# An f32 mixture-of-experts layer: products 4 and 5 of the first layer in seven blocks each, the second layer's first sum in its accumulator, and another order for the rotation

## The chip, the cores and the metric

One core of a Trainium2 chip. The time is device microseconds of one execution; below, one is a profiled execution, and three are plain runs. Engines are named as in the profile: PE is TensorE (PEld its weight loads), DVE is VectorE, ACT is ScalarE, POOL is GpSimd, SP is SyncE, which here only issues DMAs.

## The reference

4096 tokens of 512 features, f32. Each token is rotated by quaternions (a fixed 4x4 mixing M of its four groups of 128 features, with per-channel weights), sent to two of eight experts with at most 1024 slots each, passed through a two-layer network there, weighted, and added to the input.

```python
rot = cond(x)                              # quaternion rotation of the features
scores = softmax(rot @ gate_w.T)           # top 2 of 8, gates normalised
de = dispatch(rot)                         # (8 experts, 1024 slots, 512)
h  = relu(einsum('ecd,ehd->ech', de, fc1_w) + fc1_b)    # hidden size 2048
eo = einsum('ech,ehd->ecd', h, fc2_w) + fc2_b
out = x + sum_k gate_k * eo[slot of (token, k)]
```

## The kernel before

The first 80 us route the tokens. After that there are 32 stages k = (expert e, group g of 512 hidden units, g = 0 to 3). Of a stage both layers are block products of a 2x2 split, done with seven block products (numbered 0 to 6) in place of eight: the left factors are sums of weight blocks (`left1`, POOL), the right ones sums of blocks of the rotated tokens (`Slots.factors`, POOL, once an expert) or of second-layer weights (`right2`, POOL), and the products are added into the four result blocks by DVE and ACT.

**First layer** (`layer1`, L846). A product is 256x256 by 256x512. Products 0, 5 and 4 are done whole (`half`, L858): four f32 matmuls of 512 columns, each two records in the trace. Products 1 and 6, and then 3 and 2, are split once more into seven half blocks each, and done in pairs (`pair`, L878, with matmuls of 256 columns at L837 in `within`). The sums that these need come from `left_sub` (L146; four POOL operations of 128x128, L155 to L158) and `right_sub` (L162; four DVE operations of 128x256 on tile `xsub`, L170 to L173, once an expert). In the list of seven factors that each returns, entries 0, 1 and 3 on the left are raw blocks, 2, 4, 5 and 6 are sums; on the right 0, 1 and 2 are raw. The results collect in SBUF, in `beside` (h11, h21, r12) and h22: PSUM banks are added on by DVE (L892 for both halves of a bank, L905 for a bank added twice, L911, L929, L921), ACT writes the first ones with the bias and does the relus. `chain` (L811) then makes the second layer's remaining left factors s1, s2, r12 and, by `last`, s4, in DVE operations of 128x1024 (L823, L824, L825, L820).

**Second layer** (`second_layers`, L1124). For each pair of slot tiles (st0 = 0 and 2) seven products of eight matmuls of 256 columns (`product2`, L796, L800). `start` does product 0 of the next pair ahead, and adds it to the old accumulator into a tile v1 of its own. The accumulators `acc0` and `acc2` have one buffer; at an expert's first stage a new one is taken, ahead of o11, the first write.

**Order.** Nothing is scheduled automatically: every engine does its instructions in the order in which the program emits them. Two generators alternate (L1251 on): one unit of `layer1` of stage k, then one unit of the second layer of stage k - 1. I call such a pair a turn; 14 make a stage, turn i having unit i. The second layer's units for st0 = 0 lie in turns 3 to 9, those for st0 = 2 in turns 10 to 13 and, of the next stage, 0 to 2: `start` is in turns 7 and 0. After each unit `turn(n)` takes n operations from `background` (the chain, at its front; the rotation of the next expert's tokens, `Slots.steps`; weights and `Rows.store` of finished rows) and one from `fetches` (DMAs). How many is in PACE, by stage and turn. A store is an ACT scaling (L671), a POOL add onto the row (L673) and a POOL scatter (L657). POOL also gathers rows (L601, `gather_rows`, eight from turn 3 of g = 0 on), choices (L633, in g = 3), and the next expert's tokens (L694, `gather_ahead`), which SP then exchanges between partitions (`exchange`, 16 small DMAs for each part).

`first_layers` (L982) says when the sums are emitted: `TURN_OF_SUM` gives the turn of each of the four sums of the next stage's left factors (the order 2, 0, 1, 3 in turns 8, 9, 10, 13); they overwrite the sums of this stage, so each waits for PE's last use. Before, the sums for products 6 and 1 of stage k + 1 are emitted in turns 9 to 13 of stage k and those for 2 and 3 in turns 2 to 5 of their own stage; the xq gathers of an expert begin in turn 12 of g = 0 and turn 8 of g = 1, its rotation in turn 11 of g = 1 and turn 9 of g = 2.

Of the kernel before, what the change touches and what calls it, by code (L numbers as in the profile page):

```python
# [39 lines left out]
P = 128  # L40
# [26 lines left out]
def kernel(  # L67
# [78 lines left out]
    def left_sub(k, n, block):  # L146

        G = nc.gpsimd
        t = wsum.tile([P, 4, P], F32, tag=f"sub{n}", name=f"sub{n}_{k}")

        def b(m, c):
            return block[:, c, m * P : (m + 1) * P]

        steps = [
            lambda: G.tensor_tensor(t[:, 0], b(1, 0), b(1, 1), ALU.add),  # L155
            lambda: G.tensor_tensor(t[:, 1], t[:, 0], b(0, 0), ALU.subtract),
            lambda: G.tensor_tensor(t[:, 2], b(0, 0), b(1, 0), ALU.subtract),
            lambda: G.tensor_tensor(t[:, 3], b(0, 1), t[:, 1], ALU.subtract),  # L158
        ]
        return [b(0, 0), b(0, 1), t[:, 3], b(1, 1), t[:, 0], t[:, 1], t[:, 2]], steps  # L160
# [417 lines left out]
    vp = ctx.enter_context(tc.tile_pool(name="vp", bufs=1))  # L578
# [35 lines left out]
    beside = [hp.tile([P, 3, 2, HALF], F32, name=f"beside{i}") for i in range(2)]  # L614
    unused = [hp.tile([P, 2, HALF], F32, name=f"hidden{i}") for i in range(5)]
# [60 lines left out]
    class Slots:  # L676
# [37 lines left out]
        def arrivals(self, half):  # L714

            n = PER if half == 0 else 2
            t = self.a if half == 0 else self.b
            for at in range(0, PER, n):
                for st in range(n):
                    yield lambda st=st, at=at: self.gather_ahead(t[:, st], half, at + st)  # L720
                yield from [lambda: None] * 2
                for b in range(QT):
                    yield lambda b=b, at=at: self.exchange(t, half, at, b)
                yield from [lambda: None] * 2
# [71 lines left out]
    def product2(out, st0, factors, n, first, tiles=range(2)):  # L796
# [11 lines left out]
        if st0 + 2 == PER and 1 in tiles and n in (2, 3, 4, 5):  # L808
            unused.append(factors[0][n])

    def chain(k, h22):  # L811


        h11, h21, r12 = (beside[k % 2][:, i] for i in range(3))
# [3 lines left out]
        def last():  # L818
# [7 lines left out]
            *[lambda: None] * (2 if k == NK - 1 else 0),  # L826
            last,
        ]

# [16 lines left out]
    def layer1(k, factors, subs):  # L846
# [5 lines left out]
        h11, h21, r12 = (h[:, i] for i in range(3))  # L852
# [14 lines left out]
        for m in range(2):  # L867
            half(a[m], m, 0, True)
            nc.scalar.activation(h11[:, m], a[m], AF.Identity, bias=lo[:, m : m + 1])
            yield  # L870
        for m in range(2):
            half(a[m], m, 5, False)
            nc.scalar.activation(r12[:, m], a[m], AF.Identity, bias=lo[:, m : m + 1])
            if m == 1:
                nc.scalar.activation(h21[:, m], a[m], AF.Identity, bias=hi[:, m : m + 1])
            yield

        def pair(n, o, at, base, base_read):  # L878

            two = h[:, at : at + 2]
            t, u = bank1(f"t{n}_{k}"), bank1(f"u{n}_{k}")
            halves = t.rearrange("p (n s) -> p n s", n=2)

            def both(bank, i, first=False):
                within(bank[:, A], subs, n, i, first)
                within(bank[:, B], subs, o, i)

            def add(m, half):  # L890
                to = two[:, :, m, half]
                V.tensor_tensor(to, halves, to, ALU.add)  # L892

            within(base[:, A], subs, o, 1)
            within(base[:, B], subs, o, 2)
            base_read()
            both(t, 0, True)
            add(0, A)
            yield
            both(t, 5)  # L900
            add(0, B)
            both(u, 4, True)
            to = two[:, :, :, B]
            term = u.rearrange("p (n s) -> p n s", n=2).unsqueeze(2).to_broadcast([P, 2, 2, HS])
            V.tensor_tensor(to, term, to, ALU.add)  # L905
            yield
            both(t, 6)
            add(1, B)
            within(u[:, A], subs, n, 1, True)
            within(u[:, B], subs, n, 2)  # L910
            V.tensor_tensor(two[:, 0, 0], u, two[:, 0, 0], ALU.add)  # L911
            yield
            both(t, 3)
            add(1, A)
            relu(two[:, 0])

        def from5(m):
            nc.scalar.activation(h21[:, m], a[m], AF.Identity, bias=hi[:, m : m + 1])

        def from4(m):  # L920
            V.tensor_tensor(r12[:, m], b[m], r12[:, m], ALU.add)  # L921

        yield from pair(1, 6, 0, a[0], lambda: from5(0))
        yield
        h22 = unused.pop(0)
        b = [bank1(f"b{m}_{k}") for m in range(2)]
        for m in range(2):
            half(b[m], m, 4, True)
            V.tensor_tensor(h22[:, m], b[m], h21[:, m], ALU.add)  # L929
            if m == 1:  # L930
                from4(1)
                relu(h22)
            yield
        yield from pair(3, 2, 1, b[0], lambda: from4(0))
        chain(k, h22)
# [4 lines left out]
    def layer1_plain(k, w, x):  # L940
# [4 lines left out]
        h11, h21, r12 = (beside[k % 2][:, i] for i in range(3))  # L945
        h22 = unused.pop(0)
        for half in range(2):
# [6 lines left out]
            for at, i in ((at, i) for at in parts for i in range(NJ)):  # L954
# [22 lines left out]
                if half == 1 and done:  # L977
                    chain(k, h22)
# [3 lines left out]
    def first_layers():  # L982
# [43 lines left out]
        TURN_OF_SUM = {8: 2, 9: 0, 10: 1, 13: 3}  # L1026
        nxt = None
        for k in range(NK):
# [27 lines left out]
            if k:  # L1056
                for n, block, turns in (
                    (2, left_f[2], (2, 2, 3, 3)),
                    (3, w1_of[k][:, 1, 1], (4, 4, 5, 5)),
# [3 lines left out]
                if k == 1 or g == 0:  # L1063
                    for n, turns in ((6, (1, 2, 2, 3)), (2, (4, 4, 5, 5)), (3, (6, 7, 8, 9))):
# [5 lines left out]
                units = layer1(k, (left_f, xf), (dict(lefts), right_subs))  # L1070
            else:
                units = layer1_plain(k, w1_next, xs)
            for i, _ in enumerate(units):
# [3 lines left out]
                if k:  # L1077

                    if i == 8 and k + 1 < NK:
                        lefts[6], more = left_sub(k + 1, 6, left_n[6])  # L1080
                        later(more, (9, 10, 11, 12))
                        lefts[1], more = left_sub(k + 1, 1, w1_of[k + 1][:, 0, 1])
                        later(more, (10, 11, 12, 13))
                        if g == NG - 1:
                            right_subs[1], more = right_sub(xtp, e + 1, 1, xf_n[1])
                            later(more, (8, 9, 9, 12))
# [10 lines left out]
                if e + 1 < E:  # L1097

                    if (g, i) in ((0, 12 if e else 5), (1, 8)):
                        fetches.extend(nxt.arrivals(g))  # L1100
                    if (g, i) in ((1, 11), (2, 9)):
# [22 lines left out]
    def second_layers():  # L1124
# [18 lines left out]
        def start(k, st0):  # L1143
            e, g = divmod(k, NG)
            before = biases[e] if g == 0 else accs[st0]
            a = banks(f"a2_{k}_{st0}", (k, st0) == units[-1])
            v1 = vp.tile([P, 2, DB], F32, tag="v", name=f"v1_{k}_{st0}")
# [7 lines left out]
        for n, (k, st0) in enumerate(units):  # L1155
            e, g = divmod(k, NG)
            if g == 0:
                before = biases[e]
                acc = accs[st0] = ap.tile([P, 4, D], F32, tag=f"acc{st0}", name=f"acc{st0}_{e}")
            else:  # L1160
                before = acc = accs[st0]
# [83 lines left out]
        [(1, 1)] * 2 + [(0, 1)] * 4 + [(0, 0)] + [(0, 1)] * 5 + [(1, 1), (0, 0)],  # L1245
        [(1, 1)] * 4 + [(1, 1), (0, 2), (0, 0), (0, 1), (1, 1)] + [(0, 1)] * 3 + [(1, 1), (0, 0)],
        [(1, 1)] * 2 + [(2, 1)] * 2 + [(1, 2), (0, 2), (0, 0), (0, 1), (1, 1)]
        + [(0, 1)] * 3 + [(1, 1), (0, 0)],
# [63 lines left out]
```

## Time and profile before

| | us |
|---|---|
| three runs, median (lowest, highest) | 1566.23 (1565.29, 1566.28) |
| the profiled execution | 1567.49 |
| its span | 1565.7 |
| a stage from k = 2 on | 46.56 (47.12 in g = 2) |
| DVE busy in g = 0, 1, 2, 3 | 35.6, 26.9, 39.7, 39.7 |
| POOL busy in g = 0, 1, 2, 3 | 37.1, 37.7, 21.9, 35.8 |

The profile comes from the profiled execution. Busy is the time in which an engine works on an instruction; POOL's pauses ahead of a DMA that it issues (about 0.3 us) are not in it. A row of instructions gives start, duration, engine, line, operation, output<-inputs, shape; brackets hold the idle time before it and what ended it.

### The profile page before, as it was taken

What the parts mean: (1) busy time and instruction counts of PE and PEld (TensorE: products, weight loads), DVE (VectorE), ACT (ScalarE), POOL (GpSimd) and SP (SyncE); (2) the same over time, 40 slices, a digit from 0 to 9 for tenths busy, and PEclk for the clock granted to TensorE, in tenths of its full rate; (3) what the DMA queues carried; (4) which work ended last, traced back from release to release, by engine and by line L of the source; (5) the groups of instructions that cost most, each with busy time, mean ns of one, the idle gap of its engine ahead of it and who ended that gap; (6) DMA issues with size and microseconds to landing.
All of it is one profiled execution on the core that took longest, in us unless ns stands there. A gap on an engine that the chain in (4) does not pass through costs nothing.

```text
span 1565.7 us, 17505 instructions
## 1 busy us (share of the span) xinstructions
PE 1531.0 (98%) x6399; PEld 1186.9 (76%) x6399; DVE 1152.8 (74%) x1608; ACT 316.6 (20%) x446; POOL 1045.9 (67%) x1129
## 2 busy tenths in 40 slices
PE   5899999999999999999999999999999999999997
PEld 2677777877877777877877777887777877777776
DVE  6667887588866888578885888758886688866656
ACT  3222211211131211221122221221212211121110
POOL 1763687755977478865779567785687747886453
PEclk7899999999999999999999999999999999999999
DMA  8463113421335203441135311442123511321021
GB/s 325 150 215 101 55 61 122 121 81 55 96 106 144 65 28 114 124 118 55 54 95 166 96 55 32 137 130 86 55 79 115 145 41 55 114 94 67 0 82 53
DMA packets 79374, 152.18 MB, mean 97 GB/s; under 512 B 12022, under 2 KB 40950, under 8 KB 74168
## 3 DMA queue, kind: packets, MB, share of 16 engines
q1 hardware_dynamic: 56848, 90.24, 18.6%
q0 software_dynamic: 18048, 52.31, 10.8%
q10 hardware_dynamic: 4392, 8.52, 1.4%
q8 instruction: 50, 0.82, 0.2%
q14 instruction: 36, 0.29, 0.1%
HBM read 119.77 MB, written 25.23 MB: 93 GB/s over the span
## 4 chain that ended last, share of the span: by engine, by line
PE 87%; DVE 6%; DMA 2%; issue 2%; POOL 1%; another core or an unknown queue 1%; SPq 1%; POOLq 0%; DVEq 0%
PE a L800 26%; PE b L800 19%; PE t L837 13%; PE a L858 11%; PE u L837 7%; PE b L858 7%; PE b L837 2%; PE a L837 1%; DMA xb<-in_xt_dram 1%; DVE hidden L824 1%; DVE xa L771 1%; PE p L959 1%; DVE hidden L820 1%; SPq L707 1%
## 5 line engine op out<-in xcount | busy, mean ns | idle before, releaser
L800 PE MATMUL a<-t,hidden 128*128 128x256 f32 x1024 | 242.0, 379 | 0.1
L892 DVE TENSOR_TENSOR beside<-t,beside 128x512 f32<-128x512 f32 x248 | 170.3, 687 | 92.3 <-PE t L837 88.1
L800 PEld LDWEIGHTS a<-t,hidden 128*128 128x128 f32 x1024 | 194.5, 190 | 53.0 <-issue 27.5
L833 ACT ACTIVATE beside<-beside 128x1024 f32<-128x1024 f32 x62 | 65.5, 1057 | 556.8 <-DVE beside L892 535.1
L837 PE MATMUL t<-xsub,sub 128*128 128x256 f32 x496 | 128.1, 381 | 0.9 <-DVE beside L892 0.2
L800 PEld LDWEIGHTS b<-w,hidden 128*128 128x128 f32 x504 | 95.8, 190 | 39.0 <-issue 29.2
L800 PE MATMUL b<-w,beside 128*128 128x256 f32 x512 | 121.0, 379 | 0.6 <-DVE acc L1224 0.6
L800 PE MATMUL a<-t,beside 128*128 128x256 f32 x512 | 120.9, 379 | 0.0
L800 PE MATMUL a<-w,beside 128*128 128x256 f32 x512 | 120.9, 379 | 0.0
L800 PE MATMUL b<-t,hidden 128*128 128x256 f32 x504 | 119.1, 379 | 0.0
L800 PE MATMUL b<-w,hidden 128*128 128x256 f32 x504 | 119.1, 379 | 0.0
L800 PEld LDWEIGHTS b<-w,beside 128*128 128x128 f32 x512 | 97.2, 190 | 27.3 <-issue 15.8
L800 PEld LDWEIGHTS a<-w,beside 128*128 128x128 f32 x512 | 97.3, 190 | 26.4 <-issue 14.8
L858 PE MATMUL b<-x,s 128*128 128x512 f32 x248 | 116.5, 592 | 0.0
L858 PE MATMUL a<-x,s 128*128 128x512 f32 x248 | 116.5, 592 | 0.0
L858 PE MATMUL a<-xa,w 128*128 128x512 f32 x248 | 116.4, 592 | 0.0
L137 POOL TENSOR_TENSOR s<-w 128x512 f32<-128x512 f32 x31 | 39.5, 1274 | 112.5 <-PE b L858 112.5
L139 POOL TENSOR_TENSOR s<-w 128x512 f32<-128x512 f32 x31 | 39.7, 1282 | 109.7 <-PE t L837 109.6
L140 POOL TENSOR_TENSOR s<-w,s 128x512 f32<-128x512 f32 x31 | 39.4, 1272 | 107.5 <-PE t L837 96.7
L800 PEld LDWEIGHTS a<-t,beside 128*128 128x128 f32 x512 | 97.3, 190 | 13.2
L837 PEld LDWEIGHTS t<-xsub,sub 128*128 128x128 f32 x496 | 93.6, 190 | 16.3 <-DVE beside L892 3.4
L800 PEld LDWEIGHTS b<-t,hidden 128*128 128x128 f32 x504 | 95.8, 190 | 13.0
(228 smaller groups left out, 3084.9 us busy)
## 6 DMA issues: line engine op xcount, KB each, us to landing
w<-in_w_dram SPq DMA_DIRECT2D x64, 1024.0 KB
xb<-in_xt_dram SPq DMA_DIRECT2D x8, 1024.0 KB
out_dram<-in_x_dram ACTq DMA_DIRECT2D x1, 8192.0 KB
rows<-xa SPq DMA_DIRECT2D x112, 64.0 KB
rows<-xb SPq DMA_DIRECT2D x224, 32.0 KB
b<-in_b_dram POOLq DMA_DIRECT2D x8, 256.0 KB
c<-choice,slot_cho POOLq DMA_INDIRECT x64
rows<-out_dram,slot_tok POOLq DMA_INDIRECT x64
```

Of the source, the lines that this page charges most:

```text
L137: lambda: G.tensor_tensor(s[0], w[:, 1, 0], w[:, 1, 1], ALU.add),
L139: lambda: G.tensor_tensor(s[2], w[:, 0, 0], w[:, 1, 0], ALU.subtract),
L140: lambda: G.tensor_tensor(s[3], w[:, 0, 1], s[1], ALU.subtract),
L707: nc.sync.dma_start(slots_of[half][q * CW : (q + 1) * CW, at : at + t.shape[1], b * P : (b + 1) * P], t[b * CW : (b + 1) * CW, :, q * P : ...
L771: V.scalar_tensor_tensor(to, t, M[:, i, j : j + 1], to, ALU.mult, ALU.add)
L800: nc.tensor.matmul(out[m] if isinstance(out, list) else out[:, m], lhsT=factors[0][n][:, c, (st0 + m) * P : (st0 + m + 1) * P], rhs=factor ...
L820: V.tensor_tensor(s4, h21, s2, ALU.subtract)
L824: lambda: V.tensor_tensor(s2, s1, h11, ALU.subtract),
L833: nc.scalar.activation(h, h, AF.Relu)
L837: nc.tensor.matmul(out, lhsT=subs[0][n][i], rhs=subs[1][n][i], start=first, stop=True, skip_group_check=True,)
L858: nc.tensor.matmul(out, lhsT=factors[0][n][:, c, m * P : (m + 1) * P], rhs=factors[1][n][:, c, :], start=first and c == 0, stop=c == 1, sk ...
L892: V.tensor_tensor(to, halves, to, ALU.add)
```

## The change

Products 5 and 4 are done by seven blocks as well, one at a time, each with a bank of its own (t5, t4) whose two halves hold two running sums; product 0 alone stays whole. Each half sum is added by one DVE operation to both result columns that it belongs to. h22 moves into `beside`, with a copy of a half of h21 by ACT as its start, and two buffers of `unused` go. The sums for 5 are emitted in turns 0 and 1 and those for 4 in turns 6 and 7 of the stage that uses them; both share a tile. The right sums of 5 and 4 are made with the others in g = 0. v1 goes into the accumulator, which is taken in `start`. `last` is put into the background only when `product2` frees its buffer, in turn 2. The arrivals, the rotation and PACE have new places. The diff, cut:

```diff
-    beside = [hp.tile([P, 3, 2, HALF], F32, name=f"beside{i}") for i in range(2)]
-    unused = [hp.tile([P, 2, HALF], F32, name=f"hidden{i}") for i in range(5)]
+    beside = [hp.tile([P, 4, 2, HALF], F32, name=f"beside{i}") for i in range(2)]
+    unused = [hp.tile([P, 2, HALF], F32, name=f"hidden{i}") for i in range(3)]
...
-        if st0 + 2 == PER and 1 in tiles and n in (2, 3, 4, 5):
+        if st0 + 2 == PER and 1 in tiles and n in (2, 4, 5):
             unused.append(factors[0][n])
+            if n == 2 and waiting:
+                background.insert(0, waiting.pop())
...
+        def add_to_both(two, m, half, term):
+            to = two[:, :, m, half]
+            V.tensor_tensor(to, term.unsqueeze(1).to_broadcast([P, 2, HS]), to, ALU.add)
...
+        two, three = h[:, 0:3:2], h[:, 2:4]
+        t5 = bank1(f"t5_{k}")
+        singles(a[0], 5)
+        nc.scalar.activation(r12[:, 0], a[0], AF.Identity, bias=lo[:, 0:1])
+        within(t5[:, A], subs, 5, 0, True)
         yield
+        singles(a[0], 6)
+        nc.scalar.activation(h21[:, 0], a[0], AF.Identity, bias=hi[:, 0:1])
+        within(t5[:, B], subs, 5, 4)
+        add_to_both(three, 0, A, t5[:, A])
+        yield
+        t, u = bank1(f"t1_{k}"), bank1(f"u1_{k}")
+        within(t5[:, A], subs, 5, 5)
+        add_to_both(three, 0, B, t5[:, A])
+        add_twice_to_both(three, t5[:, B])
+        both(t, 1, 6, 0, True)
+        add(two, 0, A, t)
+        yield
+        within(t5[:, A], subs, 5, 6)
+        add_to_both(three, 1, B, t5[:, A])
+        both(t, 1, 6, 5)
+        add(two, 0, B, t)
+        both(u, 1, 6, 4, True)
+        add_twice(two, u)
+        yield
...
+        nc.scalar.activation(h22[:, 1], h21[:, 1], AF.Copy)
+        singles(b, 4, True)
+        V.tensor_tensor(h22[:, 0], b, h21[:, 0], ALU.add)
...
-        TURN_OF_SUM = {8: 2, 9: 0, 10: 1, 13: 3}
+        TURN_OF_SUM = {8: 2, 11: 0, 12: 1, 13: 3}
+        ARRIVE = (
...
+            {
+                (0, 3): [(0, 0)],
+                (0, 6): [(1, 0)],
+                (0, 13): [(0, 1)],
+                (1, 6): [(1, 1)],
+                (1, 10): [(1, 2)],
+                (1, 13): [(1, 3)],
+            },
...
+                lefts[5], more = left_sub(k, 5, left_f[5], 4)
+                later(more, (0, 0, 1, 1))
-                    (2, left_f[2], (2, 2, 3, 3)),
-                    (3, w1_of[k][:, 1, 1], (4, 4, 5, 5)),
+                    (2, left_f[2], (2, 3, 4, 4)),
+                    (3, w1_of[k][:, 1, 1], (4, 5, 5, 6)),
...
-                    for n, turns in ((6, (1, 2, 2, 3)), (2, (4, 4, 5, 5)), (3, (6, 7, 8, 9))):
+                    for n, turns in (
+                        (5, (0, 1, 2, 3)),
+                        (6, (2, 3, 5, 5)),
+                        (4, (5, 7, 7, 8)),
+                        (2, (8, 10, 10, 11)),
+                        (3, (7, 10, 11, 12)),
+                    ):
...
+                    if i == 6:
+                        its[4], more = left_sub(k, 4, left_f[4])
+                        later(more, (6, 6, 7, 7))
...
-                    if (g, i) in ((1, 11), (2, 9)):
+                    if (g, i) in (((1, 5), (2, 2)) if e else ((1, 11), (2, 2))):
                         background.extend(nxt.steps(g - 1))
...
-            v1 = vp.tile([P, 2, DB], F32, tag="v", name=f"v1_{k}_{st0}")
+            v1 = accs[st0][:, :2, :DB]
...
     PACE = (
-        [(1, 1)] * 2 + [(0, 1)] * 4 + [(0, 0)] + [(0, 1)] * 5 + [(1, 1), (0, 0)],
-        [(1, 1)] * 4 + [(1, 1), (0, 2), (0, 0), (0, 1), (1, 1)] + [(0, 1)] * 3 + [(1, 1), (0, 0)],
-        [(1, 1)] * 2 + [(2, 1)] * 2 + [(1, 2), (0, 2), (0, 0), (0, 1), (1, 1)]
-        + [(0, 1)] * 3 + [(1, 1), (0, 0)],
+        [(1, 1)] * 2 + [(1, 1)] * 4 + [(0, 0)] + [(0, 1)] * 5 + [(1, 1), (0, 0)],
+        [(1, 1)] * 4 + [(0, 0), (1, 1)] + [(0, 1)] * 3 + [(0, 0), (0, 1), (1, 1), (2, 1), (0, 1)],
+        [(1, 1)] * 3 + [(1, 2), (0, 0), (1, 1), (0, 0), (0, 1), (0, 1), (0, 1), (0, 1), (1, 1), (2, 1), (0, 1)],
+        [(1, 1)] * 6 + [(0, 0)] + [(0, 1)] * 4 + [(1, 2)] * 3,
     )
```

`singles(bank, n)` does blocks 1 and 2 of product n into the bank's two halves, `both(bank, n, o, i)` block i of products n and o. Unit 6 does t5's block 3, unit 7 ends the pair 1 and 6; units 8 to 11 do product 4 as 2 to 6 do product 5, beside the pair 3 and 2, which ends in unit 13. The first unit shown in the diff (`singles(a[0], 5)`) is unit 2, and each `yield` ends one. In ARRIVE, of which the table for experts after the first is shown, a key is (g, turn) and an entry (half, part): even parts are gathers, odd ones exchanges.

## The prediction

> **What bounds the kernel now.** I read the page's busy shares first, then its chain, then the stages one by one, then GpSimd's (POOL's) order of work in the stage that is fullest. The page:
>
> ```profile
> PE 1531.0 (98%) x6399; PEld 1186.9 (76%) x6399; DVE 1152.8 (74%) x1608; ACT 316.6 (20%) x446; POOL 1045.9 (67%) x1129
> ...
> PE 87%; DVE 6%; DMA 2%; issue 2%; POOL 1%; another core or an unknown queue 1%; SPq 1%; POOLq 0%; DVEq 0%
> ```
>
> TensorE is the bound. Next, the busy times of four successive stages (a stage is one pass k): g = 3 of expert 4, then g = 0, 1, 2 of expert 5. Columns: the stretch and its length; PE, PEld, DVE, ACT, POOL, each with its number of instructions; clock, DMA share, GB/s:
>
> ```profile
> 919.19:965.75 46.56, 46.56 (x193) 36.42 (x192) 39.73 (x52) 7.19 (x10) 35.81 (x36) 1.00 0.14 46
> 965.75:1012.31 46.56, 46.56 (x193) 36.48 (x192) 35.57 (x49) 9.74 (x14) 37.09 (x38) 1.00 0.35 107
> 1012.31:1058.87 46.56, 46.56 (x193) 36.48 (x192) 26.89 (x35) 12.16 (x18) 37.74 (x43) 1.00 0.49 142
> 1058.87:1105.98 47.11, 46.99 (x193) 36.31 (x192) 39.71 (x51) 9.61 (x14) 21.92 (x27) 1.00 0.25 73
> ```
>
> A stage is 46.56 us of matmuls without a gap; only g = 2 loses 0.56, where the chain of waits passes through VectorE's (DVE's) L824 and L771. So every microsecond taken from TensorE counts, as long as DVE and POOL keep up. POOL has 37 of 46.6 us in g = 0 and 1, not counting the 0.3 us ahead of each DMA it issues. POOL's instructions in time order, at the start of g = 0 and of g = 1:
>
> ```profile
> 965.50 2.36 POOL L128 TENSOR_TENSOR x<-xa,x 128x1024 f32<-128x1024 f32 x1
> 967.82 2.24 POOL L125 TENSOR_TENSOR t<-w 128x512 f32<-128x512 f32 x1
> 970.14 2.20 POOL L126 TENSOR_TENSOR t<-w,t 128x512 f32<-128x512 f32 x1
> ...
> 979.23 0.96 POOL L601 DMA_INDIRECT rows<-out_dram,slot_tok  x1 [0.15 <-issue]
> ```
>
> ```profile
> 1014.17 1.76 POOL L657 DMA_INDIRECT out_dram<-rows,slot_add  x1 [0.28 <-POOL rows L673]
> ...
> 1018.64 0.58 POOL L158 TENSOR_TENSOR sub<-w,sub 128x128 f32<-128x128 f32 x1
> 1019.19 1.27 POOL L140 TENSOR_TENSOR s<-w,s 128x512 f32<-128x512 f32 x1
> ```
>
> The L158 and L140 of the second fence belong to turn 13 of g = 0, which TensorE left at 1012.31: POOL is 8 us late there, and it costs nothing, because the next left sums that TensorE wants are those of turn 4 and later. It ends 1020.46, 54.7 us after that g = 0 began (965.75).
>
> **TensorE.** In time order 4 records of 128x512 take 1.72 us (0.4305 each), 8 of 128x256 1.72 (0.2155); an f32 matmul is two records. Products 4 and 5 were 16 records of 512, 6.89 us; seven blocks each make 28 of 256, 6.03. Gain 0.854 a stage, 31 stages: **26.5 us**, all on the path. The 0.56 of seven g = 2 stages (3.9) lies in the rotation's place, and the rotation now starts in g = 1, so I take it as gone and charge what comes instead. The stage's matmuls become 45.7 us; the turns (one unit of each layer) are 3.45, 3.45, 3.02, 3.02, 3.02, 3.88, 3.88, 2.59, 3.02, 2.59, 3.88, 3.88, 3.45, 2.59.
>
> **POOL.** Eight sub sums of 128x128 more a stage, spaced 0.415 (0.46 each): 3.3 us. What matters is when they are due. Product 5's first use in turn 2 (singles) reads the last of its four sums; they are queued in turns 0 and 1, *behind* all of the previous stage. Product 4's are due in turn 8 and queued in turns 6 and 7. In g = 0 the four gathers of xq move in at turn 3 (they ran in g = 1, after L140) and the first two of the second half at turn 9. Four of these six were behind L140 before, and now stand ahead. From g = 0's begin to the end of product 5's sums in the next stage: 54.7 us as before, + 3 x 1.66 for three sets of sums, + 4 gathers x 1.33, - 6.3 (two pauses of POOL, 4.31 and 1.99, that a late POOL has not) = 58.7, + 1 for more collisions = 59.7. TensorE wants them at 45.7 + 6.9 + 0.4 = 53.0. **Late by 6.7.** From there to turn 8: the second layer's four sums (L125 to L128) 5.0, products 2's, 3's and 4's sums 5.0, four stores of 1.28 + 0.28 + 1.0 = 10.3, collisions 1, together 21.3, against 19.4 of TensorE: late by up to 1.9 more. I take 7.5 a boundary; it occurs where the previous expert is stored and the next one gathered, e = 1 to 6 (expert 7 gathers nothing, 8 us less, in time): **45 us**. Without collisions the same sum is about 53, equal to what is wanted, so its lower bound is 0; its upper is 11 each, 66.
>
> Here the Trainium skill (SBUF — State Buffer, "Who interferes with whom") speaks against the change: a DVE instruction with two SBUF inputs and a POOL instruction that reads SBUF exclude one another for the whole instruction, and one with a single SBUF input doesn't collide. The rows agree: L892, from PSUM, has 687 ns everywhere, but L126 above takes 2.20 instead of 1.27 beside L824, and L171 1.49 instead of 0.41. POOL's excess at that start, over eight instructions, is 4.4 us, and it is within my 54.7. If the lock were taken as free the boundary would cost 0; by the rows it costs 7, and eight more xsub sums an expert can only add.
>
> The first-sum edit (v1 into acc, vp gone) moves no instruction. For g = 0 it puts the wait for the old acc's four stores on v1, in turn 0 of the next stage, with DVE's chain (s1, s2, r12) queued behind; before, the first write was in turn 3. The fourth store's POOL add will end near 55, v1 is wanted near 50: DVE stands about 4 us. Its cover is TensorE's wait for POOL at the same place, until about 60; I cost it at 0, and up to 4 if POOL is in time (never below 0: it only adds a wait).
>
> **DVE.** Layer 1 goes from 14 adds of 512 and 2 of 1024 to 20 and 4: 6 x 0.687 + 2 x 1.225 = 6.6 us a stage (rows L892, L905; broadcasting the input should not matter, as L905 broadcasts already). xsub: 8 more an expert, 0.41 to 1.49 each, in g = 0. Stage totals of g = 0 to 3: 35.6 + 6.6 + 8 x 0.7 = 48, and with some 5 us of rotation moved from g = 2 and 3 into g = 1, 39, 44 and 44, against 45.7. Alone that nearly fits; the order is what costs. Each layer 1 bank is added to, read by DVE, and added to again in the next turn, so DVE may lag about a microsecond. Turn 4 gives DVE an add (0.6 spaced), the add from t5's other half over both columns (1.15) and the add from t (0.6); turn 5 wants t back 3.45 us after turn 4's begin. With DVE free at +0.8 that ends at +3.2: no wait. In g = 2 and 3 `last` (1.2), three rotation items of 0.67 and two adds precede from turn 2 on: counted from turn 3, `last` ends +2.0 to 2.5, add 3.1, item 3.8, o11 4.4, two items 5.7, that is turn 4 + 2.7, then 2.35: +4.6 to 5.1 at worst, a wait of 1.1 to 1.6. I take 1.3, in 14 stages: **18 us** (0 to 28). g = 0 has it too, and 0.5 in turn 12 (product 3's third right sum is queued behind turn 11's adds and ends +4.35 of 3.88); both lie under POOL's lateness. ACT's extra copy (0.69) meets 10 us of 46: nothing. k = 1 has 24 xsub sums at once: 0 to 3, taken as 0 since its DVE has 30 of 43 us and POOL 21. SP's exchanges move one to two turns, ahead of the next w1 load, which is due in turn 8, 25 us on: nothing; 1 us a boundary if it were late.
>
> **Sum.** Profiled execution 1567.5 (span 1565.7): - 26.5 - 3.9 + 45 + 18 = 1600.1. The three runs' median, 1566.2, is 1.3 lower: **1599**.
>
> **Rivals.** *POOL keeps up* (not slower): collisions fall because DVE and POOL shift against one another, or the gathers go faster than 1.3. It decides below about 53 us to the end of product 5's sums. For it: the sum without collisions fits exactly, and so do DVE's stage means. Against: 4.4 us of collisions in the trace. Then 1566.2 - 30.4 + 0 to 25 of leftover waits: 1536 to 1562. *DVE alone binds*: POOL in time, but g = 0 with 48 us of work in 45.7 costs 2.3 to 4 and the others 18: 1566.2 - 30.4 + 18 + 7 x 3 = 1575. For it: DVE's total rises by 220 us to over nine tenths of the span. Against: POOL's sum is later still at the same place. *The blocks don't save*: were 256-column records dearer inside than 0.2155, nothing is won; 1566; the 256-column rows of both layers say no.
>
> A second rule, TensorE: Matmul & The Clock Gate, Part 1: an idle window of some 3.4 us halves TensorE's clock until it has been busy as long. No row here shows it: the longest stage gap is 0.56 with a clock of 1.00. By the rule a wait of 5 us in turn 2 would add up to 1.7 (one window at half speed), 10 over six boundaries; while POOL is the late one it gives POOL time, so I take 0 and put 10 into the high end.
>
> **How the numbers follow.** POOL late and turn 5 waits (1580 to 1625): 0.50. DVE alone (1564 to 1585): 0.13, of which 0.10 slower. POOL keeps up: 0.36, of which 0.01 within 0.2%. No saving: 0.01. Within 0.2% (3 us) is what a measurement of this kernel can hardly tell from no change. Faster 0.35, same 0.05, slower 0.60. Range 1542 to 1618: cases of both signs hold most of the chance, and the likeliest one's own range is 1580 to 1625.
>
> **What would show it.** Right: stages of 45.7 us plus waits; g = 0 and 1 together near 99 with PE idle before turn 2's or turn 8's matmuls, released by POOL `sub`; g = 2 and 3 near 47 with idle before L837's t, released by DVE. Wrong: g = 0 and 1 at 45.7 to 46.5 each, with POOL's product 5 sums done before turn 2. A wait of DVE on POOL rows (L673) at g = 1's v1 longer than TensorE's would make the first-sum edit the culprit.

## The result and the profile after

The changed kernel takes **1644.0 us** (median of six runs, 1640.4 to 1646.0) against 1566.2 (six runs, 1565.3 to 1568.0): 1.0493 times as long, 95% interval 1.0481 to 1.0505. Slower, as forecast, but by 77.8 us where 33 were forecast, and above the range. The span of the profiled execution (1640.4 us, the fastest of the six) grew from 1565.7 to 1638.6. Line numbers below are those of the kernel that a row is from; `within`, L837 before, is L839 in the changed kernel.

The page, busy shares and chain:

```profile
PE 1531.0 (93%) x6771; PEld 1249.5 (76%) x6771; DVE 1377.2 (84%) x1920; ACT 328.1 (20%) x477; POOL 1164.3 (71%) x1377
...
PE 55%; POOL 22%; DVE 13%; issue 5%; DMA 2%; SPq 1%; another core or an unknown queue 1%; ACT 0%; POOLq 0%; DVEq 0%; ACTq 0%
```

DVE gained 224 us (220 were foreseen) and POOL 118, and the chain of waits passes through both: 35% of it where 7% was. The same four stages as before the change, with the same columns:

```profile
966.84:1014.21 47.37, 46.35 (x205) 38.43 (x204) 42.64 (x56) 7.71 (x11) 38.13 (x44) 1.00 0.14 46
1014.21:1066.43 52.22, 47.50 (x205) 38.18 (x204) 46.85 (x66) 10.15 (x15) 47.53 (x54) 1.00 0.41 128
1066.43:1115.22 48.79, 46.33 (x205) 38.51 (x204) 38.27 (x49) 11.65 (x19) 38.42 (x46) 1.00 0.45 123
1115.22:1162.87 47.65, 46.41 (x205) 38.35 (x204) 42.76 (x57) 10.60 (x15) 24.12 (x33) 1.00 0.16 50
```

All four are longer than 46.56, g = 0 by most. What TensorE waited for shows in its instructions in time order, those with idle time ahead of them (the dots stand for rows without any). First in g = 0, which begins at 1014.21:

```profile
1028.95 0.70 PE L839 MATMUL t<-xsub,sub 128*128 128x256 f32 x2 [1.65 <-DVE beside L897]
1032.58 1.73 PE L839 MATMUL t<-xsub,sub 128*128 128x256 f32 x6 [0.33 <-DVE beside L902]
...
1050.26 0.70 PE L839 MATMUL t<-xsub,sub 128*128 128x256 f32 x2 [0.41 <-DVE beside L902]
1054.14 1.13 PE L839 MATMUL t<-xsub,sub 128*128 128x256 f32 x4 [0.16 <-DVE xsub L171]
1059.61 1.13 PE L839 MATMUL t<-xsub,sub 128*128 128x256 f32 x4 [1.75 <-DVE xsub L172]
1063.74 0.70 PE L839 MATMUL t<-xsub,w 128*128 128x256 f32 x2 [0.41 <-DVE xsub L173]
```

All six waits are for DVE: three for a bank of running sums, three for a right sum (tile `xsub`) that is made in the turn before its use. They add up to 4.7 us. The other 1.8 of the stage's 6.5 also lie at these six places: the first pair of matmuls after a wait takes 0.70 us where 0.59 is usual, and the profile counts the last one before it as 0.16 longer. In g = 1 there are two, both for POOL, at turn 2 (product 5's left sums) and turn 8 (product 4's):

```profile
1074.58 0.70 PE L839 MATMUL a<-x,sub 128*128 128x256 f32 x2 [0.66 <-POOL sub L158]
1096.13 0.70 PE L839 MATMUL b<-x,sub 128*128 128x256 f32 x2 [1.80 <-POOL sub L158]
```

In g = 2 there is one, in turn 5, and it is the one that the prediction worked out:

```profile
1132.68 1.73 PE L839 MATMUL t<-xsub,sub 128*128 128x256 f32 x6 [1.24 <-DVE beside L902]
```

Two stages fell out of the pattern: k = 1 (51.8 us where 43.46 were) and expert 7's g = 0 (54.9).

**The account.** From k = 1 to k = 30 the stages became 74.8 us longer. The matmuls account for -28.9 (0.854 in each of 30, 0.55 in each of six g = 2, where the prediction counted seven); the losses above that are:

| place | predicted | measured |
|---|---|---|
| g = 0 and g = 1 of experts 1 to 6 | 45 | 39.1 + 19.9 = 59.0 |
| g = 2 and 3, 14 stages | 18 | 25.8 |
| expert 7's g = 0 | 0 | 9.2 |
| first stage, k = 1 | 0 | 9.2 |
| k = 29 and 30 | 0 | 0.5 |
| sum | 63 | 103.7 |

### The profile page after: what moved, and what is told of

It is laid out like the page before. It is cut to its first block, busy times and chain, and to the rows that moved or that the text cites. A ratio compares the mean times of both kernels' runs of the same rounds, so it can differ in the third digit from the quotient of the medians.

```text
span 1638.6 us, 18818 instructions
## 1 busy us (share of the span) xinstructions
PE 1531.0 (93%) x6771; PEld 1249.5 (76%) x6771; DVE 1377.2 (84%) x1920; ACT 328.1 (20%) x477; POOL 1164.3 (71%) x1377
## 4 chain that ended last, share of the span: by engine, by line
PE 55%; POOL 22%; DVE 13%; issue 5%; DMA 2%; SPq 1%; another core or an unknown queue 1%; ACT 0%; POOLq 0%; DVEq 0%; ACTq 0%
PE a L799 15%; PE t L839 14%; PE b L799 12%; PE u L839 5%; PE a L860 4%; POOL rows L672 4%; POOL out_dram L656 3%; PE b L839 2%; POOL sub L155 2%; DVE beside L897 2%; POOL sub L158 2%; POOL sub L157 2%; DVE beside L902 2%; POOL rows L600 1%; PE a L839 1%
## 5 line engine op out<-in xcount | busy, mean ns | idle before, releaser
L839 PE MATMUL t<-xsub,sub 128*128 128x256 f32 x868 | 240.4, 392 | 50.3 <-DVE beside L902 21.1
L799 PE MATMUL a<-t,beside 128*128 128x256 f32 x1024 | 242.0, 379 | 0.1
L839 PEld LDWEIGHTS t<-xsub,sub 128*128 128x128 f32 x868 | 155.0, 189 | 103.9 <-DVE beside L902 35.0
L799 PEld LDWEIGHTS a<-t,beside 128*128 128x128 f32 x1024 | 194.5, 190 | 39.7 <-issue 12.7
L887 DVE TENSOR_TENSOR beside<-t,beside 128x512 f32<-128x512 f32 x248 | 170.1, 686 | 27.5 <-PE t L839 23.1
L897 DVE TENSOR_TENSOR beside<-t,beside 128x512 f32<-128x512 f32 x248 | 169.5, 683 | 23.8 <-PE t L839 19.5
L799 PE MATMUL a<-t,hidden 128*128 128x256 f32 x512 | 120.9, 379 | 0.0
L137 POOL TENSOR_TENSOR s<-w 128x512 f32<-128x512 f32 x31 | 39.5, 1275 | 111.6 <-PE t L839 111.5
L799 PEld LDWEIGHTS a<-t,hidden 128*128 128x128 f32 x512 | 97.3, 190 | 13.2
L155 POOL TENSOR_TENSOR sub<-s 128x128 f32<-128x128 f32 x124 | 79.0, 637 | 35.8 <-PE t L839 35.8
L656 POOL DMA_INDIRECT out_dram<-rows,slot_add x64 | 66.4, 1037 | 35.8 <-DVE rows L651 17.5
```

The source lines that it names most:

```text
L137: lambda: G.tensor_tensor(s[0], w[:, 1, 0], w[:, 1, 1], ALU.add),
L656: nc.gpsimd.indirect_dma_start(out=out_of[st], out_offset=bass.IndirectOffsetOnAxis(ap=slot_add[:, s : s + 1], axis=0), in_=self.rows[st], ...
L799: nc.tensor.matmul(out[m] if isinstance(out, list) else out[:, m], lhsT=factors[0][n][:, c, (st0 + m) * P : (st0 + m + 1) * P], rhs=factor ...
L839: nc.tensor.matmul(out, lhsT=subs[0][n][i], rhs=subs[1][n][i], start=first, stop=True, skip_group_check=True,)
L887: V.tensor_tensor(to, bank.rearrange("p (n s) -> p n s", n=2), to, ALU.add)
L897: V.tensor_tensor(to, term.unsqueeze(1).to_broadcast([P, 2, HS]), to, ALU.add)
```

## Experiments

The theory after the result: DVE's work in g = 0 and POOL's queue from g = 0 into g = 1 are two separate limits. Rivals: POOL alone (the prediction), the places that the change gave to work that it moved, and the first-sum edit. Each kernel was run once beside the kernel before (1564 to 1567), except where an interval is given.

### 1. Right sums of 5 and 4 only once

`right_sub` makes the right sums of products 5 and 4 for the first expert and hands out the old tiles later, so later experts' right factors are stale:

```diff
+        if n in (5, 4) and n in kept:
+            t = kept[n]
+        else:
+            t = kept[n] = pool.tile([P, 4, HS], F32, tag=f"xsub{n}", name=f"xsub{n}_{e}")
...
+        if n in (5, 4) and n in made:
+            steps = []
+        made.add(n)
```

> The changed kernel, but the right sums (xsub) of products 5 and 4 are made for the first expert only and its sums are reused by the others: 8 DVE operations less in g = 0 of experts 1 to 7; matmuls and POOL work as in the changed kernel. Theory (DVE is late in g = 0, because these sums stand in its queue ahead of adds[...]): g = 0 falls from 52.2 to about 49, expert 7's from 54.9 to about 51, other stages stay; some 25 us less, 1615. Rival (POOL is late, as the prediction had it, and DVE's waits only follow): g = 0 stays near 52, 1638.

Measured: 1637.0, g = 0 51.9, g = 1 48.75. The theory missed: this is what the rival, POOL alone, forecast, and only run 2 tells the two apart. The wait of 1.65 in turn 4 is gone, but the waits for right sums in turns 11 and 12 are 1.37 and 1.75 (0.16 and 1.75 in the changed kernel). So fewer sums did not shorten the waits there. That they are made in the turn ahead of their use is the next suspect; run 5 moves them.

### 2. No right sums after the first expert

As before, for all six products (the text of the edit has `(1, 2, 3, 4, 5, 6)`): later experts read old right sums.

> As before, but no right sum at all is made after the first expert: 20 DVE operations less in g = 0 and 4 less in g = 3. Theory: g = 0 falls to about 47, what is left being turn 5's wait and POOL's product 4 sums, due in turn 8; g = 1 keeps its 3 us or gains 1 to 2, since POOL gets less time; g = 3 falls by half a microsecond; about 1598. Rival (POOL late): g = 0 stays above 51.

Measured: 1622.9. g = 0 fell to 46.75, as the theory had it, which rules the rival out; g = 1 rose to 52 to 54, by 3 to 5 us where 1 to 2 were expected. TensorE in g = 1 of this kernel:

```profile
1065.81 0.70 PE L846 MATMUL a<-x,sub 128*128 128x256 f32 x2 [3.86 <-POOL sub L159]
...
1066.78 3.46 PE L806 MATMUL b<-w,hidden 128*128 128x256 f32 x8
...
1087.40 0.70 PE L846 MATMUL b<-x,sub 128*128 128x256 f32 x2 [0.17 <-POOL sub L159]
```

With DVE's waits out of g = 0, TensorE arrives at turn 2 earlier and stands there for POOL. g = 0 and 1 of this expert (5) together take 98.8, that is 7.4 over two matmul stages of 45.7 (over six experts the mean is 99.5). It looks like the prediction's 7.5, but only 4.0 of it are the two waits for POOL. Another 1.5 are matmuls at half rate (the records that took twice their 0.2155 us): eight that usually take 1.89 us take 3.46 a microsecond after the wait, and the granted clock of the stage is 0.97. The rest is 1.0 in g = 0 and the slow restarts. In the changed kernel the waits at these two places, 0.66 and 1.80, are followed by no such stretch.

### 3. Left sums of 5 and 4 left out

`left_sub` hands out raw weight blocks for products 5 and 4 instead of sums, so these two products are of other factors:

```diff
+        if n in (4, 5):
+            return [b(0, 0), b(0, 1), b(0, 0), b(1, 1), b(0, 0), b(0, 1), b(1, 0)], []
```

> The changed kernel without the left sums of products 5 and 4 (raw blocks stand in their place): 8 POOL operations less in every stage, matmuls and DVE the same. Theory: the first stage (51.8) falls to about 44.5, g = 1 from 48.8 to about 46, g = 0 by about 1 only (fewer collisions), g = 2 and 3 stay at 47.6 and 47.4; about 1610. Rival (POOL late): g = 0 falls to 46.5 as well, about 1575.

Measured: 1618.3. g = 1 fell to 46.3, g = 0 stayed at 52.2: DVE's loss there doesn't depend on POOL's new sums. k = 1 fell to 45.2, so the left sums are most of its loss, and it was product 5's that it waited for. k = 2 rose from 48.3 to 52.5: TensorE, earlier now, waits 2.29 in turn 2 for one of POOL's whole left sums (L138), and the matmuls behind that wait run at half rate.

### 4. Other places for rotation, stores and gathers

Rotation out of turns 1 to 3 of g = 2 and 3, g = 1's stores behind product 4's left sums, and the first expert's gathers from turn 3 of g = 1 on. The core of it:

```diff
-        [(1, 1)] * 4 + [(0, 0), (1, 1)] + [(0, 1)] * 3 + [(0, 0), (0, 1), (1, 1), (2, 1), (0, 1)],
+        [(1, 1), (1, 0), (0, 1)] + [(0, 0)] * 4 + [(0, 1)] + [(1, 1)] * 4 + [(2, 1), (1, 1)],
```

> The changed kernel with three other places and the same work: in g = 2 and 3 no rotation step in turns 1 to 3 (they follow in turns 5 to 13); in g = 1 the four stores behind product 4's left sums, with the exchanges after them and the rotation behind; in the first stage the token gathers from turn 3 on instead of ahead of the stage. Theory: g = 2 and 3 fall to about 46.3 (turn 5's wait gone), g = 1 to about 46.3, the first stage to about 45, g = 0 stays at 52; about 1600. Rival (DVE's total is the bound, 43 to 44 us in those stages): the waits come back in later turns, g = 2 and 3 stay above 47, and only g = 1 and the first stage gain, about 1615.

Measured: 1718.0 where 1600 was expected, by far the slowest. Its parts went different ways: g = 2 and 3 fell to 46.85 and k = 1 to 46.1, but g = 1 rose to 62. DVE, and under it TensorE, in that g = 1:

```profile
1148.74 0.69 DVE L1220 TENSOR_TENSOR acc<-a,b 128x512 f32<-128x512 f32 x1 [14.23 <-POOL rows L672]
```

```profile
1150.89 2.07 PE L839 MATMUL t<-xsub,sub 128*128 128x256 f32 x4 [12.81 <-DVE beside L897]
1152.75 3.49 PE L799 MATMUL b<-w,hidden 128*128 128x256 f32 x8
```

L1220 is v1 of the second half, in turn 7: in the accumulator it must wait for the last store of the old one, and DVE's adds, which TensorE wants, queue behind it. So the first-sum edit is free only while the stores stay ahead of turn 7.

### 5. Right sums one to three turns earlier

```diff
-                        (4, (5, 7, 7, 8)),
-                        (2, (8, 10, 10, 11)),
-                        (3, (7, 10, 11, 12)),
+                        (4, (5, 6, 7, 7)),
+                        (2, (7, 8, 8, 10)),
+                        (3, (7, 8, 9, 10)),
```

> The changed kernel with the right sums of products 4, 2 and 3 emitted one to three turns earlier in g = 0 (4: turns 5, 6, 7, 7; 2: 7, 8, 8, 10; 3: 7, 8, 9, 10), same work. Theory A (in g = 0 DVE is late because sums are queued behind the adds of the turn ahead of the one that wants them; POOL's queue is a second limit, which the run without right sums showed at 98.8 us for g = 0 and 1 together): expert 7's g = 0 falls from 54.9 to about 50, the others' g = 0 from 52.2 to about 49.5, and g = 1 rises, so that the two together don't fall below 98.8 from 101.0; about 1622. Theory B (the number of DVE operations[...] binds in g = 0, wherever they stand): g = 0 stays above 51.5.

Measured: 1646.6. g = 0 fell from 52.2 to 49.7, since the waits in turns 11 to 13 were gone: places matter there, as theory A has it. But g = 1 took it back: 52 to 53, with 3.78 for POOL at turn 2. Together they take 101.6 to 102.9 in five of six experts, no less than the changed kernel's 101.0. Of this, 1.7 to 2.9 us are again matmuls at half rate behind the long wait. Without them the sum would be 99.9 in each of the five (an estimate: every 256-column matmul record that took twice its 0.2155 us, put back to it), so the earlier sums gain 1 us and the one long wait costs more than that.

### 6 and 7. One product alone by blocks

Product 4 alone: product 5 whole again (its units, left and right sums as before the change). Product 5 alone: the same the other way round.

```diff
+        for m in range(2):
+            half(a[m], m, 5, False)
+            nc.scalar.activation(r12[:, m], a[m], AF.Identity, bias=lo[:, m : m + 1])
...
-                lefts[5], more = left_sub(k, 5, left_f[5], 4)
-                later(more, (0, 0, 1, 1))
```

> Half of the change: product 4 by blocks as in the changed kernel, product 5 whole as in the kernel before (no sums for 5; product 6's right sums in turns 0 to 3); order tables, v1 and arrivals of the changed kernel. Pure matmul time of a stage 46.1. Theory: without product 5's sums in turns 0 and 1 the first stage falls to about 44.5, g = 1 to about 46.3, g = 2 and 3 to about 46.2 since turn 4's list of adds is short again; g = 0 keeps the late sums of 2 and 3, about 49; 1572. Rival (the work of DVE and POOL as such is too much, half of it costs half): half of the loss, about 1605.

> The other half: product 5 by blocks, product 4 whole, the rest as in the changed kernel. Theory: the costs with a fixed place in product 5 stay: first stage 51 to 52, g = 2 and 3 near 48 (turn 5's wait on a stage of 46.1), g = 1 about 48 and g = 0 about 50; 1608. Rival: the same half as product 4 alone, about 1605 for both.

Measured: 1601.9 with product 4 alone, 1638.6 with product 5 alone. Neither theory came true (1572 and 1608); product 4 alone is at its rival's half of the loss, but product 5 alone is far from it. Product 4 costs 3.7 in g = 0 (49.8 against 46.13 us of matmuls, which is 46.56 less half of the 0.854), 2 in g = 1, 0.15 to 0.2 in g = 2 and 3, and 4.5 in k = 2. Product 5 alone has nearly the changed kernel's losses: k = 1 51.8, g = 0 52.6 to 56.4, g = 2 47.9. Only g = 1 is nearly free (46.2 to 47.1). In k = 1 TensorE waits for product 5's left sums, which come first in the stage, behind POOL's earlier queue; in g = 0 it waits for DVE alone, first for the banks (turns 4 and 5), later for the right sums of products 2 and 3.

### 8 and 9. Product 4 alone with other places

Run 8: v1 in a tile of its own again, gathers from turn 12 of g = 0 and turn 8 of g = 1, right sums earlier, stores from turn 7 of g = 1 on, rotation out of turns 1 to 3. Run 9 is the same with the stores in turns 3, 5, 7 and 8 and the changed kernel's rotation in g = 2 and 3. From the changed kernel's places to run 9's, cut:

```diff
-                (0, 3): [(0, 0)],
-                (0, 6): [(1, 0)],
+                (0, 12): [(0, 0)],
+                (1, 2): [(0, 1)],
+                (1, 8): [(1, 0)],
...
-                        (4, (5, 7, 7, 8)),
-                        (2, (8, 10, 10, 11)),
-                        (3, (7, 10, 11, 12)),
+                        (4, (4, 5, 6, 7)),
+                        (2, (6, 7, 8, 9)),
+                        (3, (7, 8, 9, 10)),
...
-            v1 = accs[st0][:, :2, :DB]
+            v1 = vp.tile([P, 2, DB], F32, tag="v", name=f"v1_{k}_{st0}")
```

> Product 4 alone by blocks, with what the runs so far point to: v1 in a tile of its own again; g = 1's stores behind product 4's left sums (turn 7 on); the token gathers in turn 12 of g = 0 and turn 8 of g = 1 as in the kernel before, the first expert's from turn 3 of the first stage; rotation from turn 8 of g = 1, none of it in turns 1 to 3 of g = 2 and 3; right sums of 6, 4, 2, 3 two turns or more ahead. Theory: g = 0 46.5 to 47, g = 1 46.3, g = 2 and 3 46.3: about 1558, faster than the kernel before. Rival (DVE's work as such): g = 0 above 48, 1575.

> The placed kernel with product 4 alone by blocks, with two things changed: the four stores in g = 1 go out in turns 3, 5, 7 and 8 (two ahead of product 4's left sums, all ahead of turn 10, in which the first write into the accumulator needs them), and the rotation in g = 2 and 3 is spread as in the changed kernel. Theory (the accumulator's single buffer pins the stores from behind as product 4's sums do from ahead, and turn 4's list is short with product 5 whole): g = 0 46.2, g = 1 46.4, g = 2 and 3 46.3; 1555, faster than the kernel before. Rival (POOL has no room for both in g = 1): g = 1 stays at 48 or above, 1565 to 1570.

Run 8 took 1617.1 where 1558 was expected: g = 0 was 46.17, but g = 1 54, since o11 in turn 10, now the first write of the new accumulator, waited 7.25 for the late stores. Its g = 2 and 3 took 47.2, not 46.3: the rotation is no better placed later. Run 9 took **1553.1** (1551.4 to 1553.5) beside 1564.0 for the kernel before, 0.9931 times, interval 0.9914 to 0.9948: a version faster than both kernels. Its g = 3, 0, 1 and 2:

```profile
912.54:958.87 46.33, 46.33 (x199) 37.45 (x198) 40.18 (x52) 7.76 (x11) 36.13 (x40) 1.00 0.15 46
958.87:1005.05 46.18, 46.18 (x199) 37.45 (x198) 39.48 (x57) 10.27 (x15) 38.97 (x43) 1.00 0.33 108
1005.05:1051.33 46.28, 46.28 (x199) 37.54 (x198) 32.12 (x43) 12.20 (x19) 39.17 (x46) 1.00 0.48 139
1051.33:1097.66 46.33, 46.33 (x199) 37.45 (x198) 38.19 (x52) 10.45 (x15) 21.61 (x31) 1.00 0.28 79
```

PE busy equals the length in every stage: no idle time is left in these four, and of the 0.43 us that product 4 saves in a stage, 0.23 to 0.38 come through. The 0.55 of each g = 2 is gone as well.

### 10. The first-sum edit alone

The kernel before, with v1 in the accumulator as the only change (a new accumulator is then taken in `start`, as in the changed kernel):

```diff
...
-            v1 = vp.tile([P, 2, DB], F32, tag="v", name=f"v1_{k}_{st0}")
+            v1 = accs[st0][:, :2, :DB]
```

> The kernel before, with only v1 kept in the accumulator (no tile of its own). Theory (v1's wait for the old accumulator's four stores lies in turns 7 and 0, where they are long done or TensorE has work queued): no difference, 1566, g = 0 and 1 at 46.6. Rival (the wait holds up DVE in front of the chain and turn 7's adds): g = 1 longer by 1 to 4 us for seven experts, 1573 to 1594.

Measured: 1564.03 against 1563.97, 1.0004 times, interval 0.9994 to 1.0014. It costs nothing by itself.

### 11. Neither right sums nor left sums of 5 and 4

Runs 2 and 3 in one kernel (stale right factors, raw left ones).

> The changed kernel with no right sums after the first expert (older ones are read again) and without the left sums of products 5 and 4 (raw blocks are read in their place): both suspects of g = 0 and g = 1 are away at once. Theory (two separate limits, DVE's right sums in g = 0 and POOL's left sums in g = 1, each of which becomes the bound when the other is taken away): g = 0 near 46.7, g = 1 near 46.3, together 93 (changed kernel 101.0; either taken away alone 98.5 to 98.8); g = 2 and 3 stay at 47.3 to 47.6 by the waits in turn 5; first stage near 45; in all 1575, 1565 to 1585. Rival (a third cost, such as the adds of the chain or the gathers themselves): g = 0 and 1 together stay above 96, in all above 1595.

Measured: 1589.4; k = 1 45.2. g = 0 and g = 1:

```profile
985.62:1033.16 47.54, 46.17 (x206) 38.59 (x204) 35.63 (x45) 10.16 (x15) 40.08 (x44) 1.00 0.43 136
1033.16:1080.57 47.41, 46.27 (x205) 38.59 (x204) 41.91 (x49) 11.77 (x19) 37.18 (x40) 1.00 0.45 125
```

Together 95.0, 2 above the theory and 1 below the rival's bound. The theory missed that waits for DVE's adds, in turn 5 of g = 0 and in turns 3 and 4 of g = 1, then cost these stages what turn 5 costs g = 2 and 3 (47.3 to 47.5 in every stage). So the rival is right in part: of the 9.6 us that the changed kernel loses in these two stages, some 3.5 remain with neither kind of sum. In steps from here, for expert 5: POOL's left sums add 3.8 (98.8, run 2), DVE's right sums 3.5 (98.5, run 3), both 6.0 (101.0, the changed kernel). Of the 3.8, 1.5 are run 2's matmuls at half rate, which the changed kernel doesn't have here; 2.3 and 3.5 come near 6.0. They nearly add up; little of either hides under the other.

### 12. Both products in the places of run 9

v1 stays in the accumulator and the stores in turns 0 to 3, as there is no room for its own tile beside product 5's. Of the edit, the right sums:

```diff
-                        (6, (2, 3, 5, 5)),
-                        (4, (5, 7, 7, 8)),
-                        (2, (8, 10, 10, 11)),
-                        (3, (7, 10, 11, 12)),
+                        (6, (1, 2, 4, 5)),
+                        (4, (4, 5, 6, 7)),
+                        (2, (6, 7, 8, 9)),
+                        (3, (7, 8, 9, 10)),
```

> The changed kernel, both products by blocks, with the places of the version that was faster with product 4 alone: gathers from turn 12 of g = 0 and turn 8 of g = 1 (first expert: from turn 3 of g = 1), the right sums of 6, 4, 2 and 3 one to three turns earlier, rotation from turn 8 of g = 1 and turn 6 of g = 2. v1 stays in the accumulator and the stores in turns 0 to 3, since there is no room for a v1 of its own beside the tiles of product 5. Theory (the two limits are DVE's and POOL's work for product 5, which has no better place, so that moving other work helps only in part): first stage 44 to 46, g = 0 near 49, g = 1 48 to 51 (its wait in turn 2 behind POOL stays), g = 2 and 3 47.3 to 47.6; in all 1615, 1598 to 1635. Rival (only the places were wrong, and both products can be had for the price of their matmuls): g = 0 and g = 1 at 46 to 46.7 each; in all below 1575.

Measured: 1643.5, above the range of the theory and no better than the changed kernel. Its g = 0 and g = 1:

```profile
1018.15:1067.88 49.73, 46.77 (x205) 38.35 (x204) 45.48 (x66) 10.15 (x15) 41.49 (x47) 1.00 0.32 101
1067.88:1120.66 52.78, 48.02 (x206) 39.66 (x204) 36.35 (x49) 11.78 (x19) 41.21 (x51) 0.97 0.45 129
```

g = 1 came out above the 48 to 51 expected: 4.57 of it is the wait for POOL in turn 2, and another 1.7 is PE busy time above 46.3, at a clock of 0.97: matmuls at half rate behind that wait, 1.5 to 2.9 us in each expert. Without them the two stages would still take 100.7 to 101.0 (an estimate as in run 5), so they don't decide the comparison. The rival (only the places were wrong) is out, for these places at least: what DVE gives back in g = 0 is lost to POOL at the next turn 2.

## Why the prediction was right in sign and wrong in size

**TensorE's saving: right.** k = 30, a stage in which PE has no idle time, takes 45.83 where 45.7 was computed.

**POOL at the boundary: its time was right, what it costs was not.** From the begin of g = 0 to the end of product 5's sums in g = 1: 59.7 predicted. POOL's instructions in time order, about there:

```profile
1068.50 1.29 POOL L140 TENSOR_TENSOR s<-w,s 128x512 f32<-128x512 f32 x1
1069.73 1.47 POOL L155 TENSOR_TENSOR sub<-s 128x128 f32<-128x128 f32 x1
...
1073.09 1.43 POOL L158 TENSOR_TENSOR sub<-s,sub 128x128 f32<-128x128 f32 x1
```

L158 ends at 1074.5, 60.3 after 1014.2. But TensorE, held up by DVE in g = 0, came for it at 59.7 and not at the 53.0 computed, so that it waited 0.66 where 6.7 were charged. The second lateness, 1.9 in turn 8, is the trace's 1.80. In run 2, with DVE's waits of g = 0 nearly gone, the wait in turn 2 is 3.86.

**"Both lie under POOL's lateness": the step that failed for g = 0.** The prediction saw that turn 5's wait and product 3's third right sum would be late in g = 0, and took them as hidden, because TensorE would wait for POOL anyway. But POOL's lateness falls in turns 2 and 8 of g = 1, after the DVE waits of g = 0. So the cover works the other way round: DVE's waits come first and cost 6.5 us, and POOL's lateness shrinks behind them, to 3.1 in all of g = 1. It doesn't shrink one for one, since DVE and POOL also hold one another up: the 5.5 us that g = 0 takes more than in run 2 take only 1.8 off g = 1, half rate aside. The sign that the prediction named, PE idle for POOL with the two stages near 99, came out as 101.0 with 2.5 of idle for POOL and 4.7 for DVE. The wait for the third right sum (0.5 predicted) is 1.75. That sum (L172, 0.41) stands behind the fourth step of another product's right sum, which took 1.91; this row of DVE and the row of POOL beside it:

```profile
1057.31 1.91 DVE L173 TENSOR_TENSOR xsub<-xb,xsub 128x256 f32<-128x256 f32 x1
```

```profile
1057.66 1.27 POOL L672 TENSOR_TENSOR rows<-acc,rows 128x512 f32<-128x512 f32 x1
```

A 0.41 us operation took 1.91 beside a POOL add: the first rule of the prediction, but at a spot where it had charged nothing. Together the two limits and the adds are 9.8 a boundary instead of 7.5 (59.0 over six).

**"Expert 7 gathers nothing, in time": wrong, 9.2 us.** POOL was in time there for g = 1 (46.2), but in g = 0, with no gathers between them, its sums and stores come back to back and starve DVE. DVE, then POOL:

```profile
1451.04 3.33 DVE L173 TENSOR_TENSOR xsub<-xb,xsub 128x256 f32<-128x256 f32 x1
```

```profile
1451.17 0.48 POOL L158 TENSOR_TENSOR sub<-s,sub 128x128 f32<-128x128 f32 x1
1451.59 1.27 POOL L137 TENSOR_TENSOR s<-w 128x512 f32<-128x512 f32 x1
1452.81 1.27 POOL L672 TENSOR_TENSOR rows<-acc,rows 128x512 f32<-128x512 f32 x1
```

DVE's end, 1454.37, comes 0.3 after that of the third POOL operation, and TensorE waits 3.17 for what follows. Without right sums this stage is 46.36 (run 2); without the new left sums it is still 54.5 (run 3).

**k = 1 taken as 0: wrong, 9.2 us.** The prediction looked at DVE's 24 right sums and at POOL's busy total, 21 of 43 us, and not at POOL's order. TensorE, then POOL, in k = 1:

```profile
91.40 1.22 PE L839 MATMUL a<-x,sub 128*128 128x256 f32 x2 [6.13 <-POOL sub L158]
```

```profile
82.42 1.79 POOL L693 DMA_INDIRECT xa<-in_xq_dram,slot_tok  x1 [0.30 <-issue]
84.51 1.95 POOL L693 DMA_INDIRECT xa<-in_xq_dram,slot_tok  x1 [0.30 <-issue]
```

Four gathers of the next expert stand ahead of product 5's last sum, due in turn 2. Leaving those sums out takes 6.6 of the 9.2 away (run 3); sending the gathers later (run 4) takes 5.7. About 1.8 of the 9.2 are matmuls at half rate after the wait (the row above takes 1.22 where 0.59 is usual): the prediction's second rule, which it had put at nothing.

**The turn 5 wait: right place, size 25.8 instead of 18.** The wait itself is 1.24, predicted 1.3. The stage loses 1.9 because PE's busy time in it is 46.41, not 45.7, and k = 2 loses 2.6. Of the 0.7, 0.27 are the longer last matmul and the slow first pair about that wait, and 0.4 are five stops of 0.05 to 0.11 us at other matmuls, most of the same `t<-xsub,sub` kind, which the sum of the prediction has no term for.

**v1 in the accumulator at 0: right** (run 10), with a price that the prediction didn't name: it forbids to move the stores behind turn 7 (run 4). The rival *DVE alone binds* is half of the truth, since DVE alone costs g = 0 6.5 us, which runs 2 and 3 show; its other half, POOL in time, is not.

## What to carry to other kernels

When two engines are both nearly full, don't let one's lateness cover the other's unless both waits fall at the same instruction: waits at different turns add up, and each engine that is relieved hands the time on to the next wait. Look for the stages that differ from the pattern (the first, the last expert's) and read their queue order, not their busy total: two of 30 stages made 18 of 104 us of loss. Look also at the length of a single wait: in runs 2, 5 and 12 one wait of about 4 us cost up to 2.9 us more than its length, and several short ones did not. And a split that saves a little on the bound engine pays only where its sums can be made well ahead of their use: product 4 alone with its sums early gave 0.7%, both products none.

## What the runs showed of the hardware

- TensorE after a long wait: the pair of matmuls that takes 0.59 in k = 1 took 1.22 right after the 6.13 us wait, and the clock of that stage is 0.93 (before: 1.00). After 12.81 us (run 4) eight matmuls took 3.49 against 1.89. Over the stages k = 1 to 30 of all the runs: after each of the 36 waits of 3.7 us or more, a stretch of matmuls at half rate followed within 1.3 us (granted clock 0.50 from 1078.9 to 1084.5 in run 5) and cost 1.5 to 2.9 us; after 218 waits of 1.0 to 1.9 us there was none. Of 22 waits between 2.0 and 3.5 us, half had it: 2.29 did (run 3, k = 2), 3.17 did not (the changed kernel, expert 7). So the second rule of the prediction has the cost about right (1.7), but the stretch also came after waits shorter than its 3.4 us. What decides between 2 and 3.5 us is not shown.
- A DVE operation with two SBUF inputs isn't merely delayed by the POOL operation under way: in expert 7's g = 0 three POOL operations came back to back, and it ended only 0.3 us after the last of them (3.33 us for 0.41 of work).
